# Transposed tokens from DRAM and a scaled row in place of TensorE transposes, in an attention and FFN kernel

## The chip, the core and the metric

The kernel runs on one core of a Trainium2 chip. The metric is device time in microseconds (us). Before the change it takes 655.53 us, the median of 3 runs (655.39 to 655.58).

A core has five engines that run at the same time, each with its own queue of instructions in order: TensorE (PE in the profile; its weight loads are PEld), VectorE (DVE), ScalarE (ACT), GpSimd (POOL) and SyncE (SP), which here issues DMAs. PE writes to PSUM banks; DVE and ACT read them.

## The reference

Tokens x are 2 x 2048 rows of D = 512. The context is 2 x 77 rows of 512. There are 16 heads of 32.

```
x = x + tanh(g_xattn) * (softmax(q k^T / sqrt(32)) v @ Wo^T + bo)
      q = layernorm(x) @ Wq^T + bq,  k = ctx @ Wk^T + bk,  v = ctx @ Wv^T + bv
      layernorm(x) = (x - mean) / sqrt(var + 1e-5), with no gain or bias
x = x + tanh(g_ffn) * qlinear(gelu(qlinear(layernorm(x), w1, b1)), w2, b2)
      qlinear(x, w, b) = (xq @ wq^T + b) * (sw * sx)
      xq, wq: rounded to 8 bits, one scale for each whole tensor
```

The query projection needs layernorm(x) with the 512 features on the partitions, while x comes with the tokens on the partitions.

## The kernel before

The 4096 tokens are 8 blocks of 512 (NB = 8, TB = 512), each of four tiles t of 128 tokens. Blocks are counted from 0 here, as in the code: x(0) to x(7). The first stage (lines 211 to 550) is attention in float32 for all blocks; the weights w1 and w2 are quantized beside it. The second stage (lines 570 to 638) computes the hidden layer in bf16, the third (lines 649 to 694) the output. The change touches only the first.

Loads are queued first (lines 115 to 136), most on SP: x of block 0, the key weights by groups of 128 columns, the query and value weights, the context, x of block 1. wk_sb and wv_sb live in buffers of the pool xblk, eight of 1 MB, through which x and the raw weight pieces of w1 and w2 also pass; a load waits on SP until its buffer is free.

*Before the loop* (lines 438 to 457) the orders of PE and DVE are written out by hand; ACT's is made by the compiler's planner. For block 0, tile by tile: statistics (layernorm_stats), 1/sigma on POOL (L163, a power of -0.5), transpose_x, and project_k(0, g), the keys of head group g for the first batch element. project_k multiplies wk by the context into a bank (pk) and then places 32 rows for each of four heads, with the bias added, into kblk: for b = 0 all four by ACT (L235), for b = 1 alternately by DVE (L237) and ACT.

*In the loop* (lines 463 to 523) PE's order alone is by hand; the planner orders the other engines from its costs and the order of the program. tc.issue_after(ins) puts the instructions of its block behind ins on the queue of the same engine. Each block i has eight steps s, two for each head group g. A step has, in PE's order:

- at even s, apply_v of the group before (pc, L345), which multiplies the transposed softmax by the values;
- softmax(i, s + 2), two steps ahead: scores ps on PE (L299), maximum mx and difference e on DVE (L308, L312), exponential on ACT (L318), sum and reciprocal on DVE (L320, L322), and the product e * rs on POOL (L323);
- transpose_a twice: PE transposes the softmax of step s (pta, L336), ACT copies it to aT (L337);
- at even s, project_o(i - 1, g) (po, L358), added to x by DVE (L365);
- at odd s, project_q: at 1 and 3 groups 2 and 3 of this block, at 5 and 7 groups 0 and 1 of the next (pq, L280, 8 records for four products of 128 features; copied with bias to qT by ACT, L288).

The layer norm of the next block runs beside this: norm(i + 1) at s = 1 (statistics on DVE, L159 to L162; 1/sigma on POOL, L163), and transpose_x(i + 1, t) for tiles 0 and 1 at the end of s = 3, for 2 and 3 at s = 5 ahead of the scores. transpose_x subtracts the mean and scales on DVE (xn, L266), transposes four 128x128 pieces on PE into a bank (ptx, L271), and copies them on ACT into xnT (L272).

In block 0 also: the keys and values of batch element 1 (project_k(1, s - 3) at s = 3 to 6, project_v(1) at 6). Other work of the loop: add_bias (L275, POOL), weight_step (maxima of w1 in block 1 and of w2 in block 3, quantization in 2 and 4, on DVE), and at s = 7 norm2_stats and norm2_max (DVE), the second layer norm of the block before. project_q, project_k, project_v, apply_v, project_o and scale_of share the PSUM pool ps_p, tag "pp", of two banks in turn. x of block i + 2 is queued on SP at the end of block i.

Of the kernel before, what the change touches and what calls it, by code (L numbers as in the profile page):

```python
# [15 lines left out]
P = 128  # L16
D = 512
# [25 lines left out]
def tile_flamingo_gated_block(  # L43
    ctx: ExitStack,
    tc: tile.TileContext,
    x: bass.AP,
    ctxT: bass.AP,
    g_xattn: bass.AP,
    g_ffn: bass.AP,
# [45 lines left out]
    ctx_sb = awts.tile([P, B, KC, NK], F32, name="ctx_sb")  # L95
# [3 lines left out]
    bv_sb = work.tile([NK, D], F32, tag="cT", name="bv_sb", bufs=7)  # L99
    bq_sb = const.tile([P, KC], F32, name="bq_sb")  # L100
    bk_sb = const.tile([P, KC], F32, name="bk_sb")
    tg = const.tile([P, 2], F32, name="tg")
# [7 lines left out]
        engine.dma_start(dst[:, :, c], kchunks(src)[:, :, c])  # L110

    def load_ctx(engine, b):
        engine.dma_start(ctx_sb[:, b, :, :], kchunks(ctxT[b]))

    load_x(0, pieces=NT, engines=(nc.sync, nc.scalar))
    load_ctx(nc.scalar, 0)
# [12 lines left out]
    for b in range(1, B):  # L129
        load_ctx(nc.sync, b)  # L130
    load_x(1)
    nc.sync.dma_start(wo_sb, kchunks(woT))
# [3 lines left out]
    nc.sync.dma_start(b1_sb, b1)  # L136

    ident = const.tile([P, P], F32, name="ident")
    make_identity(nc, ident)
# [71 lines left out]
    with actx:  # L211
# [7 lines left out]
        def project_k(b, g):  # L219

            pk = ps_p.tile([P, 512], F32, tag="pp", name=f"pk{b}_{g}")
            for kc in range(KC):
                nc.tensor.matmul(
                    pk[:, :NK],
                    wk_sb[:, kc, g * P : (g + 1) * P],
                    ctx_sb[:, b, kc, :],
                    start=(kc == 0),
                    stop=(kc == KC - 1),
                )
            for j in range(HG):  # L230
                r = slice(j * DK, (j + 1) * DK)
                dst = kblk[b][r, g, j % RT * NK : (j % RT + 1) * NK]
                bias = bk_sb[r, g : g + 1]
                if j % 2 or b == 0:
                    nc.scalar.activation(dst, pk[r, :NK], AF.Identity, bias=bias)  # L235
                else:
                    nc.vector.tensor_scalar(dst, pk[r, :NK], bias, None, ALU.add)  # L237

        def project_v(b):

            pv = ps_p.tile([P, 512], F32, tag="pp", name=f"pvv{b}")
            for kc in range(KC):
                nc.tensor.matmul(  # L243
                    pv[:NK, :],
                    ctx_sb[:, b, kc, :],
                    wv_sb[:, kc, :],
                    start=(kc == 0),
                    stop=(kc == KC - 1),
                )
            nc.vector.tensor_tensor(vblk[b], pv[:NK, :], bv_sb, ALU.add)  # L250

        ln, xnT, qT, aT, cT, es = {}, {}, {}, {}, {}, {}

        def norm(i):
# [3 lines left out]
            layernorm_stats(X[i], mv, rstd, f"a{i}")  # L258
            ln[i] = mv, rstd

        def transpose_x(i, t):
            mv, rstd = ln[i]
            if t == 0:
                xnT[i] = work.tile([P, KC, TB], F32, tag="xnT", name=f"xnT{i}", bufs=1)
            xn = work.tile([P, D], F32, tag="xn", name=f"xn{i}_{t}")
            nc.vector.tensor_scalar(  # L266
                xn, X[i][:, t, :], mv[:, t, 0:1], rstd[:, t : t + 1], ALU.subtract, ALU.mult
            )
            pt = ps_t.tile([P, KC, P], F32, tag="pt", name=f"ptx{i}_{t}")
            for kc in range(KC):  # L270
                nc.tensor.transpose(pt[:, kc, :], xn[:, kc * P : (kc + 1) * P], ident)  # L271
            nc.scalar.copy(xnT[i][:, :, t * P : (t + 1) * P], pt)  # L272
# [4 lines left out]
        def project_q(i, g):  # L277
            pq = ps_p.tile([P, TB], F32, tag="pp", name=f"pq{i}_{g}")
            for kc in range(KC):
                nc.tensor.matmul(  # L280
                    pq,
                    wq_sb[:, kc, g * P : (g + 1) * P],
                    xnT[i][:, kc, :],
                    start=(kc == 0),
                    stop=(kc == KC - 1),
                )
            qT[i, g] = work.tile([P, TB], F32, tag="qT", name=f"qT{i}_{g}", bufs=5)
            nc.scalar.activation(qT[i, g], pq, AF.Identity, bias=bq_sb[:, g : g + 1])  # L288

        def softmax(i, s):  # L290
# [144 lines left out]
                if j < 2:  # L435
                    load_w("w2", w2_piece, [j + 2])

        ordered = {mybir.EngineType.DVE, mybir.EngineType.PE}
        with tc.manual_schedule(engines=ordered):
            ln[0] = (  # L440
                small.tile([P, NT, 2], F32, tag="mv", name="mv0"),
                small.tile([P, NT], F32, tag="rstd", name="rstd0"),
            )
            for t in range(NT + 1):
# [12 lines left out]
            project_k(0, NG - 1)  # L457
        actx.enter_context(tc.manual_schedule(engines={mybir.EngineType.PE}))
        softmax(0, 0)
        softmax(0, 1)  # L460
        project_q(0, 1)
        project_v(0)
        for i in range(NB):
            for s in range(2 * NG):
                g, odd = divmod(s, 2)
                if not odd and s > 0:
                    apply_v(i, g - 1)
                elif not odd and i > 0:
                    apply_v(i - 1, NG - 1)
                if s == 5 and i + 1 < NB:  # L470
                    for t in (2, 3):
                        transpose_x(i + 1, t)
                if s + 2 < 2 * NG:
                    last = softmax(i, s + 2)
                elif i + 1 < NB:
                    last = softmax(i + 1, s + 2 - 2 * NG)
                for u in range(2):
                    transpose_a(i, s, u)
                if i == 0 and s == 2:


                    with tc.issue_after(last["ACT"]):
                        nc.scalar.activation(tg, tg, AF.Tanh)
                    with tc.issue_after(last["POOL"]):
                        nc.gpsimd.tensor_scalar(bo_sb, bo_sb, tg[:, 0:1], None, ALU.mult)
                if not odd and i > 0:
                    project_o(i - 1, g)
                if s in (1, 3):
                    project_q(i, g + 2)
                elif odd and i + 1 < NB:  # L490
                    project_q(i + 1, g - 2)
                if i + 1 < NB:
                    if s == 1:
                        with tc.issue_after(last["DVE"]):
                            norm(i + 1)
                    if s == 3:
                        for t in (0, 1):
                            transpose_x(i + 1, t)
                if i == 0 and 3 <= s < 7:
                    for b in range(1, B):  # L500
                        project_k(b, s - 3)
# [35 lines left out]
        xq0 = work.tile([P, NT, D], BF16, tag="xnT", name="xq0", bufs=1)  # L537
        for t in range(NT):
            v, vq = xs0[:, t, :], xq0[:, t, :]
            if t < NT // 2:  # L540
# [216 lines left out]
```

## Time and profile before

| | us |
|---|---|
| median of 3 runs | 655.53 |
| the profiled execution | 655.2 |
| its span, first to last instruction | 653.3 |
| xn on DVE (L266), 32 operations, mean 0.66 | 20.4 |
| transposes of x on PE (ptx, L271), 128 | 18.4 |
| copies of them on ACT (L272), 32 | 17.3 |
| query projection on PE (L280), 256 records | 115.4 |
| softmax product on POOL (L323), 64 of 1.23 | 78.6 |

The profile is of one execution. "Busy" counts an instruction's own duration; matmuls overlap, so their durations add up to more than the path they take. In a list of groups, a line reads: source line, engine, operation, what is written <- what is read, shapes, count, busy time and mean; in a timeline: start, length, the same names, and in brackets how long the engine was idle before and which instruction released it. The mean granted TensorE clock is 0.987 of full speed.

### The profile page before, as it was taken

To read this page: it belongs to the slowest core of one execution; us is meant where nothing else is said; L and a number is where in the kernel's file an instruction comes from. 1 tells how busy PE (TensorE), PEld (TensorE's weight loads), DVE (VectorE), ACT (ScalarE), POOL (GpSimd) and SP (SyncE) were. 2 spreads that over 40 slices of the span, in tenths; PEclk is the share of its full clock that TensorE was granted. 3 is DMA by queue.
4 is the path that set the end of the run, shared out by engine and by line. 5 is a ranking of instruction groups with operands and counts; after the bars stand their busy time and mean duration, and the time that the engine had idled before them with its cause. 6 is when DMAs were issued, how large, how long until landed. Compare 5 with 4: busy or idle time off the path is not lost.

```text
span 653.3 us, 8220 instructions
## 1 busy us (share of the span) xinstructions
PE 625.0 (96%) x3048; PEld 317.4 (49%) x3048; DVE 514.7 (79%) x809; ACT 342.8 (52%) x479; POOL 204.1 (31%) x161
## 2 busy tenths in 40 slices
PE   5999999999999999999999999599999979999997
PEld 4565555455554554555555543244444434444443
DVE  3586687998998998976877768899999788887551
ACT  4465444444444354354344441399999979544430
POOL 2144333234343334233242331000000009996000
PEclk9999999999999999999999999699999989999999
DMA  9902000031131131100000000089999109789952
GB/s 281 376 34 93 37 1 1 2 129 65 65 130 68 62 129 64 66 1 0 1 2 0 2 18 0 19 295 319 333 323 329 25 8 359 273 325 345 334 207 80
DMA packets 44255, 84.90 MB, mean 130 GB/s; under 512 B 18795, under 2 KB 22891, under 8 KB 38584
## 3 DMA queue, kind: packets, MB, share of 16 engines
q1 hardware_dynamic: 43112, 83.70, 36.5%
q10 hardware_dynamic: 1104, 0.69, 0.3%
q8 instruction: 24, 0.39, 0.3%
q14 instruction: 15, 0.12, 0.1%
HBM read 49.25 MB, written 31.46 MB: 124 GB/s over the span
## 4 chain that ended last, share of the span: by engine, by line
PE 85%; DVE 11%; ACT 2%; issue 1%; DMA 1%; POOL 0%; ACTq 0%; DVEq 0%
PE pf L674 17%; PE ph L610 17%; PE po L358 15%; PE pq L280 14%; PE pta L336 8%; PE ps L299 6%; PE pc L345 4%; PE ptx L271 2%; DVE tm L380 1%; DVE xf L189 1%; PE pvv L243 1%; DVE mx L308 1%; DVE e L312 1%; DVE sm L320 1%; DVE max_w L401 1%
## 5 line engine op out<-in xcount | busy, mean ns | idle before, releaser
L323 POOL TENSOR_TENSOR e<-e,rs 128x616 f32<-128x616 f32 x64 | 78.6, 1229 | 223.3 <-DVE rs L322 149.1
L280 PE MATMUL pq<-xnT,wq_sb 128*128 128x512 f32 x256 | 115.4, 593 | 0.9 <-ACT xnT L272 0.9
L674 PE MATMUL pf<-w2q,hq 128*128 128x512 bf16 x512 | 113.6, 385 | 2.3 <-DVE hq L205 2.0
L358 PE MATMUL po<-wo_sb,cT 128*128 128x512 f32 x256 | 114.8, 593 | 0.0
L610 PE MATMUL ph<-xqT,w1q 128*128 128x512 bf16 x512 | 112.1, 382 | 0.7 <-DVE xqT L550 0.7
L617 ACT ACTIVATE G<-ph,b1s,s 128x512 f32<-128x512 f32 x128 | 99.6, 778 | 14.1 <-PE ph L610 3.3
L337 ACT COPY aT<-pta 77x512 f32<-77x512 f32 x128 | 68.1, 582 | 69.2 <-PE pta L336 69.2
L318 ACT ACTIVATE e<-e 128x616 f32<-128x616 f32 x64 | 45.9, 717 | 85.8 <-DVE e L312 84.3
L627 DVE TENSOR_REDUCE hmax<-G 128x1 f32<-128x1024 f32 (+1 forms) x65 | 76.8, 1198 | 7.0 <-ACT G L617 6.9
L674 PEld LDWEIGHTS <-hq 128*128 128x128 bf16 x512 | 50.7, 99 | 64.9 <-issue 3.6
L610 PEld LDWEIGHTS <-w1q 128*128 128x128 bf16 x512 | 50.4, 99 | 62.2 <-issue 1.9
L336 PE MATMUL pta<-ident,e 128*77 128x128 f32 x512 | 70.2, 280 | 0.4 <-ACT xnT L272 0.4
L358 PEld LDWEIGHTS po<-wo_sb,cT 128*128 128x128 f32 x256 | 46.4, 190 | 48.2 <-issue 46.6
L320 DVE TENSOR_REDUCE sm<-e 128x8 f32<-128x616 f32 x64 | 50.6, 790 | 24.4 <-ACT e L318 24.1
L308 DVE TENSOR_REDUCE mx<-ps 128x8 f32<-128x616 f32 x64 | 50.2, 784 | 24.4 <-PE ps L299 23.9
L280 PEld LDWEIGHTS pq<-xnT,wq_sb 128*128 128x128 f32 x256 | 46.1, 190 | 47.1 <-issue 46.1
L667 ACT ACTIVATE Gb<-Gb,inv_h 128x2048 f32<-128x2048 f32 x22 | 43.7, 2001 | 36.8 <-DMA Gb<-h 32.5
L336 PEld LDWEIGHTS pta<-ident,e 128*77 128x77 f32 x512 | 55.6, 147 | 11.8 <-issue 10.3
L299 PEld LDWEIGHTS ps<-kb,qT 64*128 64x128 f32 x512 | 36.0, 186 | 43.5 <-ACT qT L288 20.6
L688 POOL TENSOR_TENSOR x<-x,b_sb 128x512 f32<-128x512 f32 x32 | 56.2, 1794 | 0.1
L312 DVE TENSOR_TENSOR e<-ps,mx 128x616 f32<-128x616 f32 x64 | 50.9, 796 | 2.4
L299 PE MATMUL ps<-kb,qT 64*128 64x154 f32 x512 | 50.6, 317 | 0.3 <-ACT qT L288 0.2
(89 smaller groups left out, 590.6 us busy)
## 6 DMA issues: line engine op xcount, KB each, us to landing
h<-G SPq DMA_DIRECT2D x22, 1024.0 KB, 5.9
Gb<-h SPq DMA_DIRECT2D x22, 1024.0 KB, 7.9
raw_w<-in_w2T SPq DMA_DIRECT2D x8, 1024.0 KB, 5.2
out_y<-x SPq DMA_DIRECT2D x32, 256.0 KB, 2.8
x<-in_x SPq DMA_DIRECT2D x7, 1024.0 KB, 5.5
raw_w<-in_w1T SPq DMA_DIRECT2D x4, 1024.0 KB, 12.6
wk_sb<-in_wkT SPq DMA_DIRECT2D x4, 256.0 KB, 5.2
wq_sb<-in_wqT SPq DMA_DIRECT2D x4, 256.0 KB, 6.2
```

The source lines that it names most:

```text
L280: nc.tensor.matmul(pq, wq_sb[:, kc, g * P : (g + 1) * P], xnT[i][:, kc, :], start=(kc == 0), stop=(kc == KC - 1),)
L299: nc.tensor.matmul(ps[:, q, u * RK : (u + 1) * RK], qT[i, g][r, t * P : (t + 1) * P], kblk[i // NBB][r, g, :], start=True, stop=True,)
L312: last["DVE"] = nc.vector.tensor_tensor(e.rearrange("p u (q r k) -> p q u r k", q=NR, r=RT), sc, mx[:, :, :, :, None].to_broadcast([P, NR, ...
L320: nc.vector.tensor_reduce(sm, e4, AX.X, ALU.add)
L323: last["POOL"] = nc.gpsimd.tensor_tensor(e4, e4, rs[:, :, :, None].to_broadcast([P, 2, HG, NK]), ALU.mult).ins
L336: nc.tensor.transpose(pt[:NK, j, :], es[i, s][:, u, j, :], ident)
L337: nc.scalar.copy(aT[i, g][:, :, t * P : (t + 1) * P], pt[:NK, :, :])
L358: nc.tensor.matmul(po, cT[i, g][:, t * P : (t + 1) * P], wo_sb[:, g, :], start=(g == 0), stop=(g == NG - 1),)
L610: nc.tensor.matmul(ph, w1q[:, kc, fc * P : (fc + 1) * P], cur[:, kc, :], start=(kc == 0), stop=(kc == KC - 1),)
L617: nc.scalar.activation(G[:, 2 * v + u, :], ph, AF.Gelu, bias=b1s[:, fc : fc + 1], scale=s1,)
L627: nc.vector.tensor_reduce(hmax[:, k + u : k + u + 1], G[:, 2 * v + u : 2 * v + u + n, :], AX.XY, ALU.max, apply_absolute_value=True,)
L674: nc.tensor.matmul(po[t], hq[:, fc, t * P : (t + 1) * P], w2q[:, fc, :], start=(fc == 0), stop=(fc == FC - 1),)
```

## The change

The host also gives x transposed (xT, 512 x 4096). For blocks 1 to 7:

- load_xT brings the block, features on the partitions, into xT_sb, in buffers of the tag xnT, now two;
- norm writes the four columns of 1/sigma to a row in DRAM and reads that row back into all 128 partitions (rrow), both DMAs on SP; it is called at s = 0, in block 0 at s = 1 as before;
- scale_x multiplies xT_sb by the row in place on POOL, four operations of 128x512, two at s = 2 and two at s = 3 (in block 0 at 3 and 4), each pair behind that step's softmax product;
- the mean is not subtracted from x; center_wq (block 0, s = 3, after the last query projection of block 0) takes from the query weights their mean over the features instead: three additions on POOL, one product with ones on PE (bank pm of "pp"), four operations on DVE that read pm and write wq_sb.

So transpose_x is left only for block 0. Before the loop ACT's order is by hand too, the keys of b = 0 are placed by DVE, and key group 2 is multiplied before the first query projection. The context lives in two buffers of the tag cT; qT has four buffers, not five. x and xT of block i + 2 are queued at s = 6.

```
+    def load_xT(i):
+        xT_sb[i] = work.tile([P, KC, TB], F32, tag="xnT", name=f"xT{i}", bufs=2)
+        nc.sync.dma_start(xT_sb[i], kchunks(xT[:, i * TB : (i + 1) * TB]))
...
-                if j % 2 or b == 0:
+                if j % 2 and b > 0:
                     nc.scalar.activation(dst, pk[r, :NK], AF.Identity, bias=bias)
                 else:
                     nc.vector.tensor_scalar(dst, pk[r, :NK], bias, None, ALU.add)
...
+            row = rows.tile([NT, P], F32, tag="row", name=f"row{i}")
+            nc.sync.dma_start(row.rearrange("t p -> p t"), rstd)
+            rstd_row[i] = work.tile([P, TB], F32, tag="rrow", name=f"rrow{i}", bufs=1)
+            nc.sync.dma_start(
+                rstd_row[i], row.rearrange("(o t) p -> o (t p)", o=1).to_broadcast([P, TB])
+            )
+
+        def scale_x(i, kc):
+
+            xs = xT_sb[i][:, kc, :]
+            nc.gpsimd.tensor_tensor(xs, xs, rstd_row[i], ALU.mult)
+
+        def center_wq():
+
+            total = work.tile([P, D], F32, tag="xn", name="wq_total")
+            nc.gpsimd.tensor_tensor(total, wq_sb[:, 0, :], wq_sb[:, 1, :], ALU.add)
+            for kc in range(2, KC):
+                nc.gpsimd.tensor_tensor(total, total, wq_sb[:, kc, :], ALU.add)
+            pm = ps_p.tile([P, D], F32, tag="pp", name="pm")
+            nc.tensor.matmul(pm, ones, total, start=True, stop=True)
+            for kc in range(KC):
+                w = wq_sb[:, kc, :]
+                nc.vector.scalar_tensor_tensor(w, pm, -1.0 / D, w, ALU.mult, ALU.add)
...
-                    xnT[i][:, kc, :],
+                    (xnT if i == 0 else xT_sb)[i][:, kc, :],
...
-        ordered = {mybir.EngineType.DVE, mybir.EngineType.PE}
+        ordered = {mybir.EngineType.DVE, mybir.EngineType.PE, mybir.EngineType.Activation}
...
-                if t > 1:
-                    project_k(0, t - 2)
+                if t in (2, 3):
+                    pk[t - 2] = project_k(0, t - 2)
+            place_k(0, 0, pk[0])
+            pk[2] = project_k(0, 2)
+            place_k(0, 1, pk[1])
             project_q(0, 0)
-            project_k(0, NG - 1)
+            place_k(0, 2, pk[2])
+            pk[3] = project_k(0, 3)
+            place_k(0, 3, pk[3])
...
-                if s == 5 and i + 1 < NB:
-                    for t in (2, 3):
-                        transpose_x(i + 1, t)
...
-                    if s == 1:
+                    first = 1 if i == 0 else 0
+                    if s == first:
                         with tc.issue_after(last["DVE"]):
                             norm(i + 1)
-                    if s == 3:
-                        for t in (0, 1):
-                            transpose_x(i + 1, t)
+                    if s in (first + 2, first + 3):
+                        with tc.issue_after(last["POOL"]):
+                            for kc in range(2 * (s - first) - 4, 2 * (s - first) - 2):
+                                scale_x(i + 1, kc)
+                    if i == 0 and s == 3:
+                        center_wq()
...
+                if s == 6 and i + 2 < NB:
+                    load_x(i + 2)
+                    load_xT(i + 2)
...
-            if i + 2 < NB:
-                load_x(i + 2)
```

More of the change, by code (lines that the diff above doesn't have):

```diff
@@ L46, in tile_flamingo_gated_block @@
     x: bass.AP,
+    xT: bass.AP,
     ctxT: bass.AP,
@@ L94, in tile_flamingo_gated_block @@
     wo_sb = awts.tile([P, KC, D], F32, name="wo_sb")
-    ctx_sb = awts.tile([P, B, KC, NK], F32, name="ctx_sb")
     kblk = [awts.tile([P, NG, RK], F32, name=f"kb{b}") for b in range(B)]
@@ L99, in tile_flamingo_gated_block @@
     bv_sb = work.tile([NK, D], F32, tag="cT", name="bv_sb", bufs=7)
+    ctx_sb = [work.tile([P, KC, NK], F32, tag="cT", name=f"ctx{b}", bufs=7) for b in range(B)]
     bq_sb = const.tile([P, KC], F32, name="bq_sb")
@@ L112, in load_ctx @@
     def load_ctx(engine, b):
-        engine.dma_start(ctx_sb[:, b, :, :], kchunks(ctxT[b]))
+        engine.dma_start(ctx_sb[b], kchunks(ctxT[b]))
     load_x(0, pieces=NT, engines=(nc.sync, nc.scalar))
@@ L131, in tile_flamingo_gated_block @@
     load_x(1)
+    xT_sb = {}
+    def load_xT(i):
+        xT_sb[i] = work.tile([P, KC, TB], F32, tag="xnT", name=f"xT{i}", bufs=2)
+        nc.sync.dma_start(xT_sb[i], kchunks(xT[:, i * TB : (i + 1) * TB]))
     nc.sync.dma_start(wo_sb, kchunks(woT))
@@ L136, in tile_flamingo_gated_block @@
     nc.sync.dma_start(b1_sb, b1)
+    rows = ctx.enter_context(tc.tile_pool(name="rows", bufs=2, space=bass.MemoryType.DRAM))
     ident = const.tile([P, P], F32, name="ident")
@@ L225, in project_k @@
                     wk_sb[:, kc, g * P : (g + 1) * P],
-                    ctx_sb[:, b, kc, :],
+                    ctx_sb[b][:, kc, :],
                     start=(kc == 0),
@@ L229, in project_k, with place_k @@
                 )
+            return pk
+        def place_k(b, g, pk):
             for j in range(HG):
@@ L244, in project_v @@
                     pv[:NK, :],
-                    ctx_sb[:, b, kc, :],
+                    ctx_sb[b][:, kc, :],
                     wv_sb[:, kc, :],
@@ L250, in project_v @@
             nc.vector.tensor_tensor(vblk[b], pv[:NK, :], bv_sb, ALU.add)
+        rstd_row = {}
         ln, xnT, qT, aT, cT, es = {}, {}, {}, {}, {}, {}
@@ L263, in transpose_x @@
             if t == 0:
-                xnT[i] = work.tile([P, KC, TB], F32, tag="xnT", name=f"xnT{i}", bufs=1)
+                xnT[i] = work.tile([P, KC, TB], F32, tag="xnT", name=f"xnT{i}", bufs=2)
             xn = work.tile([P, D], F32, tag="xn", name=f"xn{i}_{t}")
@@ L286, in project_q @@
                 )
-            qT[i, g] = work.tile([P, TB], F32, tag="qT", name=f"qT{i}_{g}", bufs=5)
+            qT[i, g] = work.tile([P, TB], F32, tag="qT", name=f"qT{i}_{g}", bufs=4)
             nc.scalar.activation(qT[i, g], pq, AF.Identity, bias=bq_sb[:, g : g + 1])
@@ L443, in tile_flamingo_gated_block @@
             )
+            pk = {}
             for t in range(NT + 1):
@@ L453, in tile_flamingo_gated_block @@
                     transpose_x(0, t - 1)
-                if t > 1:
-                    project_k(0, t - 2)
+                if t in (2, 3):
[3 more added lines that the diff above has]
+            place_k(0, 1, pk[1])
             project_q(0, 0)
-            project_k(0, NG - 1)
+            place_k(0, 2, pk[2])
+            pk[3] = project_k(0, 3)
+            place_k(0, 3, pk[3])
         actx.enter_context(tc.manual_schedule(engines={mybir.EngineType.PE}))
+        load_xT(1)
         softmax(0, 0)
@@ L492, in tile_flamingo_gated_block @@
                 if i + 1 < NB:
[L493 removed]
+                    first = 1 if i == 0 else 0
+                    if s == first:
                         with tc.issue_after(last["DVE"]):
                             norm(i + 1)
[L496 to L498 removed]
+                    if s in (first + 2, first + 3):
[4 more added lines that the diff above has]
+                        center_wq()
                 if i == 0 and 3 <= s < 7:
                     for b in range(1, B):
[L501 removed]
+                        place_k(b, s - 3, project_k(b, s - 3))
                         if s == 6:
@@ L536, in tile_flamingo_gated_block @@
         s_x, inv_x = scale_of(diagonal_of(xmax, "x"), "x", ps_p, "pp")
-        xq0 = work.tile([P, NT, D], BF16, tag="xnT", name="xq0", bufs=1)
+        xq0 = work.tile([P, NT, D], BF16, tag="xnT", name="xq0", bufs=2)
         for t in range(NT):
@@ L727 @@
         "x": x.reshape(-1, D),
+        "xT": x.reshape(-1, D).T,
         "ctxT": np.asarray(ctx_1024).transpose(0, 2, 1),
```

## The prediction

> **What bounds the kernel now.** I read the page's busy shares first, then its 40 slices, then the stages around the change, then TensorE's order of work in one block.
>
> ```profile
> PE 625.0 (96%) x3048; PEld 317.4 (49%) x3048; DVE 514.7 (79%) x809; ACT 342.8 (52%) x479; POOL 204.1 (31%) x161
> PE   5999999999999999999999999599999979999997
> DVE  3586687998998998976877768899999788887551
> ```
>
> TensorE (PE) is busy 96% of the span and is full from slice 1 to slice 23, which is the attention part. So there a removed TensorE instruction should shorten the time. The stage table (start and end, then length, and for each engine busy us and instructions) says the same and shows the neighbours:
>
> ```profile
> 0.00:20.00 20.00, 11.89 (x62) 9.35 (x64) 6.08 (x18) 8.45 (x20) 4.54 (x13) 1.00 1.00 297
> 150.00:200.00 50.00, 49.96 (x253) 25.91 (x251) 46.48 (x77) 22.21 (x38) 17.73 (x14) 1.00 0.23 85
> ```
>
> Columns are PE, PEld, DVE, ACT, POOL. In 150 to 200 us PE works 49.96 of 50 us, but VectorE (DVE) is close behind with 46.48, so DVE's lag has to be watched. POOL has room (17.73). The first 20 us hold 8 us of idle PE. TensorE's timeline in block 1 prices the transposes that go:
>
> ```profile
> 75.45 3.60 PE L280 MATMUL pq<-xnT,wq_sb 128*128 128x512 f32 x8
> 78.98 1.06 PE L345 MATMUL pc<-aT,vb 77*32 77x512 f32 x8
> ...
> 86.82 3.60 PE L280 MATMUL pq<-xnT,wq_sb 128*128 128x512 f32 x8
> 90.26 1.04 PE L271 MATMUL ptx<-ident,xn 128*128 128x128 f32 x8
> 91.23 1.07 PE L345 MATMUL pc<-aT,vb 77*32 77x512 f32 x8
> 93.88 3.60 PE L358 MATMUL po<-wo_sb,cT 128*128 128x512 f32 x8
> 97.32 1.04 PE L271 MATMUL ptx<-ident,xn 128*128 128x128 f32 x8
> 98.28 0.79 PE L299 MATMUL ps<-kb,qT 64*128 64x154 f32 x8
> ```
>
> From pq to pc takes 3.53 us without transposes (75.45 to 78.98) and 4.41 with eight (86.82 to 91.23): eight transposes cost 0.88 us of the path. With po the figures are 4.40 and 3.52 (81.64 to 85.16), again 0.88. An instruction's own 0.27 us is no price; the distance is.
>
> **What the Trainium skill says.** "TensorE: Matmul & The Clock Gate", Part 2 (step 5): the drain of one matmul overlaps the fill of the next, so a stream costs spacing, not latency. The trace agrees: 0.11 us per transpose by distance. "GPSIMD Engine Reference", 3.1: a two-input elementwise operation takes about 2.6 cycles an element at 1.2 GHz, an estimate of 1.1 us plus dispatch for 512. The trace has the same shape as what scale_x does, the bias add of L275, at 1.27 us; I use that. "DMA: Bandwidth & Descriptors", Rules for kernel authors: a non-contiguous last dimension becomes one descriptor per element, so the row of 512 values goes out as 512 descriptors; no such store is in the trace. "Advanced Engine Details and Errata", VectorE Performance Modes: GpSimd and VectorE's two-port mode block each other. The trace fits: xn (L266) takes 0.49 to 1.44 us.
>
> **The change part by part.** The profiled execution took 655.2 us with a span of 653.3; the median of the runs is 655.53, 0.3 above, so I take the sum off 655.5.
>
> *Transposes, blocks 1 to 6 (for x of blocks 2 to 7).* Two groups of 0.88 us a block: 6 x 1.76 = **-10.6 us**, all on PE's path. With them go four xn per block on DVE (0.66 us each) and four copies on ACT (0.59), beside PE.
>
> *GpSimd scaling.* Four operations of 1.27 us a block, 5.1 us on POOL. POOL then does 8 x 1.22 + 4 x 1.27 + 2 x 1.28 + 5.1 = 22.5 us in a block of about 45.6 (47.3 now, less 1.76). Free if they don't delay the softmax products (L323), which PE transposes next. These lines are of block 3; its step 5 transposes start at 194.79:
>
> ```profile
> 184.54 1.22 POOL L323 TENSOR_TENSOR e<-e,rs 128x616 f32<-128x616 f32 x1 [2.75 <-DVE rs L322]
> 185.72 1.28 POOL L275 TENSOR_TENSOR x<-x,bo_sb 128x512 f32<-128x512 f32 x1
> 190.03 1.31 POOL L323 TENSOR_TENSOR e<-e,rs 128x616 f32<-128x616 f32 x1 [3.04 <-ACT aT L337]
> 194.79 1.10 PE L336 MATMUL pta<-ident,e 128*77 128x128 f32 x8
> ```
>
> The first product is of softmax step 4, behind which the first pair of scale_x is queued; the second is of step 5, with 194.79 - 191.34 = 3.4 us to spare. A pair (2.5 us) fits into the gap 185.8 to 190.0 if the row of 1/sigma is there.
>
> *The row: norm one step earlier, two DMAs on SP.* In block 3 norm may start after e at 170.34, so at 171.1; now it starts at 174.24 and its ve_a ends at 180.70, 6.5 us. The row then follows: 177.6, rstd on POOL 1.3 (L163), store and load with two issues of 0.5. The store is unseen: 2.8 us is the landing of a 256 KB store (out_y), 5.0 to 6.2 that of the 2 KB loads bq and bk at a busy time; I take 3.5. The load into 128 partitions: 3.3, as b_sb's 256 KB. The row lands at about 186.8. The latest harmless time: product 5 must end by 194.79 - 0.88 = 193.9, less 1.3 and a pair 2.5, so 190.1. Margin 3.3 us. Not every block will have it: DVE has norm2's 3.6 us of statistics and about 5 us of maxima just before, and the w2 pieces (5.2 us to land) share SP and the DMA engines. I put 0.3 us on each of six blocks, **+1.8** (bounds 0 and the rival below). A gain below nothing is excluded: nobody waits for POOL to be busier.
>
> *Block 0.* Step 3: project_q(0,3), then the new pm matmul, pk, then pc. The pool "pp" has two banks, so pc takes pm's bank and waits for four DVE operations that read it. As L365 (0.74 us with a PSUM input) they need 2.9 us. From the end of pq: pm is one 128x512 f32 product (two records at 0.44), done at +1.05; four operations to +4.0, with 0 to 2.6 us of softmax work in front. Now pc comes 0.88 + 0.86 = 1.8 us after pq. So pc comes 2.2 to 4.8 us later; I take **+3.2**, the removed first group counted. Behind pc wait ps and all else on PE. The three adds of GpSimd (3 x 1.27) need only the loaded weights, and POOL idles before 24.57 us, so they cost nothing; placed at step 3 they would add about 4 us. Step 5: a group of 0.88 goes, with the 0.36 us wait before pta at 50.10: **-1.2**. But project_q(1,0) needs the second pair of scale_x, queued behind the product of softmax(0,6). Now ps of that softmax starts at 45.47 and its product ends at 51.7, +6.2; the pair ends at +8.7. project_q would start at +4.2 (51.01 - 45.47, less 1.32) and wants its last quarter at +6.9: **+1.8** (0 to 2.5). Together +3.8.
>
> *The first keys.* Now copy x of the last tile waits behind kb on ACT: pq starts at 15.08, after the copy of 14.44 to 15.03. With kb on DVE (0.29 us each, idle there from 10.8) the copy can follow its transposes at 13.4 and end at 14.0; PE does pk 2 first, to about 14.1. So pq starts about 14.1: **-1.0** (0 to -1.2; nothing if the loads are late, the DMA share being 1.00 there).
>
> *Loads.* xT adds 7 MB and the row loads 1.8 MB. The DMA share is 0.10 to 0.23 in the middle, and an x block lands in 5.5 us. The first xT is queued on SP before x of block 2 and the w1 pieces, whose first maximum is taken only at 79.6 us; a later x moves from the end of a block to step 6, with its xT behind it, and is wanted two steps (2 x 5.9 us) later. Nothing, at 0.4 us an issue. With ctx, three of cT's seven buffers are held in block 0, where cT fills one every other step; of qT's four at most three are alive. Nothing.
>
> Sum: -10.6 + 1.8 + 3.8 - 1.0 = **-6.0**, so 649.5 us.
>
> **Rivals.** *All is hidden* (chance 0.18): DVE takes pm's operations at once and the row is early. Then -10.6 - 1.0 and block 0 at about -1, so 643. For it: between 40 and 360 us PE now idles under 2 us, so the engines around it do keep up. Against it: pp has only two banks.
>
> *DVE takes the bound* (0.13): norm at step 0 falls into DVE's densest stretch. In block 3 the ps of step 0 ends at 165.08 and its mx starts at 169.52, 4.4 us late. If DVE's lag grows by the 3.6 us of norm there, PE waits about 1 us a block: -6.0 + 5 = about 654.5. Against it: over a block DVE loses 2.2 to 2.6 us, PE only 1.76.
>
> *The row comes late* (0.17), the slower one: POOL stands at scale_x waiting for the row, and the softmax products stand behind it. With norm ending no earlier than now (180.7), and DMAs of 5.0 and 5.2, the row lands at 180.7 + 1.3 + 11.2 = 193.2, 3.1 us past 190.1. In the five blocks with norm2 ahead (2 to 6) this is 15.5 us: 649.5 + 15.5 = 665. The decision point is 6.0 / 5 = 1.2 us past the limit, 191.3. That SP has a waiting weight load ahead of the row (it is in-order) would do the same.
>
> **How the numbers follow.** Forecast 649.5 (own range 646.5 to 652), 0.52; all hidden 0.18; DVE bound 0.13; late row 0.17. 0.2% (1.3 us) is about what the measurement can tell. Of the DVE case about half (0.06) is still faster. So faster 0.76, same 0.07, slower 0.17. The range 642.5 to 656.5 leaves out most of the late row and little else.
>
> **What would show it.** Period of blocks 5 and 6 (pc to pc, now 47.3) at 45.5 to 45.9. A PE wait before pc at step 3 of block 0 put down to the new DVE operation, 2 to 5 us. A wait in the first pq of block 1 for scale_x. The first pq at 14.1. Waits of pta for POOL stay under 3 us in all. The prediction is wrong if POOL shows long waits for the row's DMA with pta behind them, or if mx lags further in steps 0 to 2.

## The result, and the profile after

The changed kernel takes 673.05 us, the median of 4 runs (671.87 to 676.7), against 655.56 (4 runs) for the kernel before on the same chip: a ratio of 1.027 (95% interval 1.0255 to 1.029), slower. The profiled execution took 673.24 us with a span of 671.5, so it is 18.2 us of span that have to be found. The forecast was 649.5, its range 642.5 to 656.5.

The page of the kernel after, TensorE's busy row and then the slices of TensorE, of VectorE and of the granted TensorE clock:

```profile
PE 625.2 (93%) x2938; PEld 313.0 (47%) x2938; DVE 509.7 (76%) x801; ACT 323.8 (48%) x435; POOL 243.3 (36%) x192
...
PE   5999999998997998997989999599999979999997
...
DVE  5675677996985996973866867899998878888541
...
PEclk9998999998998998998999999789999998999999
```

110 records went from TensorE, yet its busy time is the same, since others took longer (the transposes of the softmax 0.292 us each on the mean, 0.280 before), and its row, full of nines in slices 1 to 23 before, has holes now: slices 9, 12, 15 and 18 in blocks 2 to 5, and 20 in block 6. At the first four VectorE and the clock have a dent in the same slice, at slice 20 the clock has none. A dent of VectorE suggests that it waits too; the lists of waits below decide that. The stage table (start and end, length, then PE, PEld, DVE, ACT, POOL, each with its instructions, then clock, DMA share and GB/s) says it in numbers:

```profile
0.00:20.00 20.00, 12.63 (x51) 10.13 (x51) 9.62 (x30) 3.63 (x5) 6.05 (x15) 1.00 1.00 293
150.00:200.00 50.00, 45.70 (x221) 23.83 (x218) 42.04 (x68) 19.13 (x32) 23.20 (x18) 0.97 0.29 101
```

From 150 to 200 us TensorE works 45.70 of 50 us (49.96 before). A block is measured from the first apply_v (pc) of one block to that of the next. Undisturbed, block 1 shows what the removal is worth. TensorE's timeline has the pc at the start of block 1 and the one at the start of block 2, first in the kernel before:

```profile
67.61 1.06 PE L345 MATMUL pc<-aT,vb 77*32 77x512 f32 x8
...
114.84 1.06 PE L345 MATMUL pc<-aT,vb 77*32 77x512 f32 x8
```

and then in the kernel after, with the second pc of block 1 between them:

```profile
73.86 1.07 PE L382 MATMUL pc<-aT,vb 77*32 77x512 f32 x8
...
85.23 1.06 PE L382 MATMUL pc<-aT,vb 77*32 77x512 f32 x8
...
119.35 1.06 PE L382 MATMUL pc<-aT,vb 77*32 77x512 f32 x8
```

114.84 - 67.61 = 47.23 us, and 119.35 - 73.86 = 45.49 us. All blocks, from the same lines of both kernels (and of the best version, which comes last in the experiments):

| block | 1 | 2 | 3 | 4 | 5 | 6 |
|---|---|---|---|---|---|---|
| before, us | 47.23 | 48.45 | 47.34 | 48.44 | 47.36 | 47.23 |
| after, us | 45.49 | 51.62 | 51.30 | 51.03 | 51.34 | 47.48 |
| last experiment, us | 45.50 | 46.69 | 46.44 | 46.70 | 45.49 | 45.49 |

Blocks 2 and 4 hold 1.2 us more in all three kernels (the scale of a weight, pg_w). Beyond that and 45.49, blocks 2 to 5 after are 4.92, 5.81, 4.33 and 5.85 us too long: 20.9 us. The lists of waits, TensorE's and GpSimd's (us in total, times, longest), give the first reason:

```profile
PE pta L373 <- POOL e L360: 15.0, 5, 4.4
...
PE ps L336 <- ACT qT L325: 2.1, 2, 1.9
...
PE pc L382 <- DVE wq_sb L296: 1.5, 1, 1.5
...
PE pq L317 <- POOL xT L284: 0.8, 1, 0.8
```

```profile
POOL xT L284 <- DMA rrow<-row: 46.8, 7, 9.6
```

TensorE waits 15.0 us for the softmax product, and GpSimd waits 46.8 us for the row, once for each of the seven blocks of x that it scales. TensorE waits behind it in blocks 2 to 5 only; one of its five waits, 0.9 us in block 3, stays in runs where the row is early (below). Why the row is late stands in the list of DMA issues (the last number is the median time from issue to landing):

```profile
rrow<-row SPq DMA_DIRECT2D x7, 256.0 KB, 5.9
...
row<-rstd SPq DMA_DIRECT2D x7, 2.0 KB, 8.3
```

The store of 2 KB takes longer than the load of 256 KB. Block 2 in the timeline, from 1/sigma to the transposes that wait:

```profile
132.41 1.02 POOL L171 TENSOR_TENSOR rstd<-ve_a,mhalf 128x4 f32<-128x4 f32 x1
133.46 0.36 SPq L275 DMA_DIRECT2D row<-rstd  x1
141.81 0.33 SPq L277 DMA_DIRECT2D rrow<-row  x1
148.78 2.49 POOL L284 TENSOR_TENSOR xT<-xT,rrow 128x512 f32<-128x512 f32 x2 [6.54 <-DMA rrow<-row]
149.24 0.20 DVE L359 RECIPROCAL rs<-sm 128x8 f32<-128x8 f32 x1
151.22 1.26 POOL L312 TENSOR_TENSOR x<-x,bo_sb 128x512 f32<-128x512 f32 x1
152.44 1.22 POOL L360 TENSOR_TENSOR e<-e,rs 128x616 f32<-128x616 f32 x1
153.72 1.99 PE L373 MATMUL pta<-ident,e 128*77 128x128 f32 x8 [3.43 <-POOL e L360]
```

The load is issued only when the store has landed, 8.35 us after it (141.81 - 133.46), and the pair of scale_x starts 6.97 us later: 15.3 us from the end of 1/sigma. The product's own input rs was ready at 149.44; it runs 3.0 us later, because the pair and a bias add are ahead of it on GpSimd's queue. TensorE stands still for 3.43 us. And there is a second reason in the last line: the eight transposes take 1.99 us instead of 1.10. TensorE comes back from the wait at a lower clock. In the table of stretches (columns as in the stage table), the clock stands at 0.50 for these 2 us:

```profile
153.70:155.70 2.00, 1.99 (x9) 1.99 (x10) 1.04 (x1) 0.58 (x1) 2.00 (x1) 0.50 0.95 350
```

The sum from the trace: before block 0's first pc +1.2; block 0 +5.05; transposes -1.74 in each of six blocks, -10.4; the excess of blocks 2 to 5 +20.9; block 6 another +2.0; the rest of the kernel -0.3. Together +18.4, against 18.2 measured.

### The profile page after: what moved, and what is told of

Same layout as the page of the kernel before. It is cut to its first block, busy times and chain, and to the rows that moved or that the text cites. A ratio compares the mean times of both kernels' runs of the same rounds, so it can differ in the third digit from the quotient of the medians.

```text
span 671.5 us, 8017 instructions
## 1 busy us (share of the span) xinstructions
PE 625.2 (93%) x2938; PEld 313.0 (47%) x2938; DVE 509.7 (76%) x801; ACT 323.8 (48%) x435; POOL 243.3 (36%) x192
## 2 busy tenths in 40 slices
DMA packets 52654, 94.07 MB, mean 140 GB/s; under 512 B 22715, under 2 KB 26811, under 8 KB 46984
## 4 chain that ended last, share of the span: by engine, by line
PE 65%; DVE 24%; POOL 4%; issue 4%; ACT 2%; DMA 1%; POOLq 0%; DVEq 0%; ACTq 0%
PE pf L720 17%; PE ph L656 16%; PE po L395 9%; PE pq L317 8%; PE pta L373 6%; PE ps L336 3%; DVE e L349 3%; DVE mx L345 3%; PE pc L382 3%; DVE xf L197 2%; DVE sm L357 2%; DVE tm L417 2%; DVE st_a L167 2%; DVE x L402 1%; DVE st_f L167 1%
## 5 line engine op out<-in xcount | busy, mean ns | idle before, releaser
L663 ACT ACTIVATE G<-ph,b1s,s 128x512 f32<-128x512 f32 x128 | 99.5, 777 | 14.1 <-PE ph L656 3.2
L317 PE MATMUL pq<-xT,wq_sb 128*128 128x512 f32 x224 | 103.5, 604 | 0.9 <-POOL xT L284 0.8
L373 PE MATMUL pta<-ident,e 128*77 128x128 f32 x512 | 74.7, 292 | 15.0 <-POOL e L360 15.0
L373 PEld LDWEIGHTS pta<-ident,e 128*77 128x77 f32 x512 | 59.3, 155 | 26.8 <-POOL e L360 17.7
L317 PEld LDWEIGHTS pq<-xT,wq_sb 128*128 128x128 f32 x224 | 41.6, 197 | 42.9 <-issue 39.2
L284 POOL TENSOR_TENSOR xT<-xT,rrow 128x512 f32<-128x512 f32 x28 | 36.9, 1338 | 46.8 <-DMA rrow<-row 46.8
L336 PE MATMUL ps<-kb,qT 64*128 64x154 f32 x512 | 51.2, 320 | 2.1 <-ACT qT L325 2.1
```

Of the source, the lines that this page charges most:

```text
L317: nc.tensor.matmul(pq, wq_sb[:, kc, g * P : (g + 1) * P], (xnT if i == 0 else xT_sb)[i][:, kc, :], start=(kc == 0), stop=(kc == KC - 1),)
L336: nc.tensor.matmul(ps[:, q, u * RK : (u + 1) * RK], qT[i, g][r, t * P : (t + 1) * P], kblk[i // NBB][r, g, :], start=True, stop=True,)
L373: nc.tensor.transpose(pt[:NK, j, :], es[i, s][:, u, j, :], ident)
L663: nc.scalar.activation(G[:, 2 * v + u, :], ph, AF.Gelu, bias=b1s[:, fc : fc + 1], scale=s1,)
```

## The experiments

The theory after the result: the row of 1/sigma is late, since its store takes 8.3 us, and GpSimd's waiting scale_x holds up the softmax product. The rivals: VectorE's denser order at step 0 makes everything late and the row's wait is only where it shows; the wait itself is harmless and the 2.5 us of scaling in front of the product is what costs; and the size of the row, not the form of its store, makes the round trip slow.

**Norm a step earlier (e1_norm_early).** The row is asked for earlier instead of being made faster.

```
-                    if s == first:
+                    if i == 0 and s == 1:
                         with tc.issue_after(last["DVE"]):
-                            norm(i + 1)
+                            norm(1)
+                if s == 7 and i + 2 < NB:
+                    with tc.issue_after(last["DVE"]):
+                        norm(i + 2)
...
+                if s == 4 and i + 2 < NB:
+                    load_x(i + 2)
                 if s == 6 and i + 2 < NB:
-                    load_x(i + 2)
                     load_xT(i + 2)
```

> norm of block i + 2 moves to step 7 of block i (two steps of a block earlier than in the change: it was called at step 0 of block i + 1, and DVE finished it at about step 2), and the load of x to step 4; norm(1) stays. Late row (theory): the row lands before step 2, POOL's waits for it in blocks 1 to 6 go to nearly nothing, PE's 15.0 us of waits for the softmax product and the slow-clock stretches behind them go, and the time falls by about 20 us to 650 to 654. GpSimd's own work (rival): the 5.1 us of scaling a block are unchanged, so the time stays above 668. DVE (rival): norm is now ahead of norm2 in the densest stretch of DVE, so the time stays at 673 or rises.

Measured: 676.26 us, ratio 1.032 (1.0294 to 1.0346). A miss. The row's wait is gone in all blocks but block 0 (GpSimd waits once, 6.8 us), but norm and norm2 now stand together at step 7. Timeline of this kernel, VectorE and then TensorE in the next block:

```profile
127.48 0.99 DVE L197 TENSOR_SCALAR xf<-x,mean,rstd 128x512 f32<-128x512 f32 x2
128.39 1.27 DVE L417 TENSOR_REDUCE tm<-xf 128x1 f32<-128x512 f32 x2
129.58 0.28 DVE L179 TENSOR_SCALAR diag_w<-ident,m_w 128x128 f32<-128x128 f32 x1
130.00 0.77 PE L186 MATMUL pg_w<-diag_w,ones 128*128 128x128 f32 x2 [5.94 <-DVE xmax L421]
```

The small product pg_w of a weight's scale waits 5.94 us for diag_w, which VectorE does only after norm2's xf and tm, and the same happens in block 4. Blocks 3 and 5 take 51.2 and 51.3 us, with a wait of 1.9 us for the exponential in each. So late VectorE work is a real cost where norm is put into a dense stretch, but here it took the place of the row's wait: this run says nothing against the late row, and doesn't show what the row costs.

**No wait for the row (e2_no_row_wait).** scale_x multiplies by bo_sb, which has long been there. It leaves out 1/sigma; instructions and DMAs stay the same.

```
-            nc.gpsimd.tensor_tensor(xs, xs, rstd_row[i], ALU.mult)
+            nc.gpsimd.tensor_tensor(xs, xs, bo_sb, ALU.mult)
```

> Both DMAs of the row stay, but GpSimd scales xT by bo_sb, which is there from the start, in place of the row; 1/sigma is left out of the queries of blocks 1 to 7. All work of POOL, DVE and the DMA queues is kept, only the wait for the row is taken away. Late row: about 650 (673 less the 22.9 us that blocks 2 to 6 lost beyond their transposes). GpSimd's own work or DVE's lag: 668 to 673, since nothing of either changed.

Measured: 654.29 us in one run, span 652.5: 19.0 us of span less than after, with norm still at step 0. TensorE's waits of this kernel:

```profile
PE ps L336 <- ACT qT L325: 1.8, 2, 1.6
...
PE pta L373 <- POOL e L360: 0.9, 1, 0.9
```

Of the 15.0 us 0.9 is left, in block 3. So VectorE's order at step 0 isn't the cause, and four operations a block of GpSimd's scaling are hidden as priced. What is missing to 649.5 is in block 0 (36.32 us), in block 6 (3.4 us above 45.49) and at the head, which is 2.6 us longer than in the kernel before.

**The wait without the work (e3_wait_only).** scale_x multiplies one column of 512, so it waits for the row as before but holds GpSimd for 0.33 us a pair, not 2.49. It leaves out the scaling of the other columns.

```
-            nc.gpsimd.tensor_tensor(xs, xs, rstd_row[i], ALU.mult)
+            nc.gpsimd.tensor_tensor(xs[:, 0:1], xs[:, 0:1], rstd_row[i][:, 0:1], ALU.mult)
```

> scale_x waits for the row as in the change but multiplies one column of each chunk only, so the queries of blocks 1 to 7 lack 1/sigma in nearly all tokens; GpSimd has almost none of the 5.1 us of scaling a block left. Late row: POOL still waits about 45 us for the row; the product behind it comes 2.5 us earlier, so PE's waits of 3 to 4 us shrink to about 1 and the clock no longer falls: 655 to 662. GpSimd's own work: the loss goes entirely, 646 to 650. DVE: 673.

Measured: 654.34 us in one run, span 652.5, just below what was expected of the late row (655 to 662) and far above the 646 to 650 of GpSimd's own work. TensorE's and GpSimd's waits of this kernel:

```profile
PE pta L373 <- POOL e L360: 4.5, 4, 2.0
```

```profile
POOL xT L284 <- DMA rrow<-row: 45.1, 7, 9.3
```

GpSimd still waits 45.1 us for the row, and TensorE only 4.5. Blocks 2 to 5 take 47.47, 47.41, 46.83 and 49.24 us: of the 20.9 us too many, 6.6 are left with the wait alone, and 0.9 with the work alone (e2). Most of the loss needs both: work that has been held back by a wait runs in front of the product just when that is due.

**The row stored as it lies (e4_row_16B).** 1/sigma lies as 128 partitions x 4 values. The change stores it in the order of the tokens, as 512 pieces of 4 bytes; here each partition's four values go out as one piece of 16 bytes. The values then stand in another order, so tokens get each other's 1/sigma.

```
-            row = rows.tile([NT, P], F32, tag="row", name=f"row{i}")
-            nc.sync.dma_start(row.rearrange("t p -> p t"), rstd)
+            row = rows.tile([P, NT], F32, tag="row", name=f"row{i}")
+            nc.sync.dma_start(row, rstd)
...
-                rstd_row[i], row.rearrange("(o t) p -> o (t p)", o=1).to_broadcast([P, TB])
+                rstd_row[i], row.rearrange("(o p) t -> o (p t)", o=1).to_broadcast([P, TB])
```

> The row is stored as it lies, 16 bytes from each partition (128 pieces in place of 512 of 4 bytes), and read back in that order, so tokens take each other's 1/sigma. If the 8.3 us of the store are paid by piece: it lands in about 3.5 to 4.5 us, the row comes 4 us earlier, PE's waits for the product fall from 15 to under 3 us, and the time is 652 to 656. If the 8.3 us are fixed (a write to DRAM and its acknowledgment): the store stays at 8 us and the time at 670 to 675.

Measured: 652.63 us in one run, span 650.8: 20.7 us less than after. The DMA issues of this kernel, and TensorE's wait:

```profile
rrow<-row SPq DMA_DIRECT2D x7, 256.0 KB, 4.5
...
row<-rstd SPq DMA_DIRECT2D x7, 2.0 KB, 1.4
```

```profile
PE pta L373 <- POOL e L360: 0.9, 1, 0.9
```

The same 2 KB land in 1.4 us. The profile counts 49966 DMA packets in this kernel and 52654 in the changed one, 2688 fewer, which is 7 x (512 - 128): the pieces are as the layouts say. Blocks 2 to 5 take 46.70, 46.43, 46.70 and 45.50 us. The 0.9 us of block 3 stay with the row early (here and in e2), so the late row accounts for 20.9 - 0.9 = 20.0 us of the changed kernel.

**A quarter of the row (h1_quarter_row).** Only tile 0's 1/sigma is stored, 128 pieces of 4 bytes, and all four tiles are scaled by it, so the 1/sigma of the other three is left out. It parts the number of pieces from their size.

```
-            nc.sync.dma_start(row.rearrange("t p -> p t"), rstd)
+            nc.sync.dma_start(row.rearrange("o p -> p o"), rstd[:, 0:1])
...
```

> Only tile 0's 1/sigma is stored (128 pieces of 4 bytes in place of 512), read back into 128 partitions as 512 bytes each, and used for all four tiles of a block. The mended row has 128 pieces of 16 bytes and lands in 1.4 us, the change's 512 pieces of 4 bytes in 8.3. If the number of pieces sets the landing: 1.4 to 2.2 us. If the size of 4 bytes does: about 8. The time falls to about 652 in the first case and stays near 670 in the second.

Measured: 665.92 us in one run, span 664.1. DMA issues and TensorE's wait:

```profile
rrow<-row SPq DMA_DIRECT2D x7, 64.0 KB, 5.5
...
row<-rstd SPq DMA_DIRECT2D x7, 0.5 KB, 7.1
```

```profile
PE pta L372 <- POOL e L359: 9.4, 5, 3.3
```

With the same number of pieces as e4 (the packets are 49966 in both) and a quarter of its bytes, the store takes 7.1 us at the median. Four times as many add 1.2. So it is stores in pieces of 4 bytes that are slow here, not 512 of them. A shorter row would have mended little: 1.2 us of 8.3.

**The head alone (f1_head_only).** The kernel before with only the new order of the first keys (project_k split into place_k, VectorE places, group 2 multiplied before the first query projection, ACT's order by hand before the loop).

> The kernel before with the edit ahead of the loop alone: the first keys placed by DVE, ACT's order by hand, key group 2 ahead of the first query projection. By the prediction's step: 1.0 us faster (ratio 0.9985), the first query projection starting at 14.1. If what the profile of the changed kernel shows is of the edit (TensorE stays at half clock some 4 us longer, first query projection at 16.0): 1 to 2 us slower (1.002 to 1.003). If the later clock is chance: no difference beyond the interval.

Measured: 655.08 against 655.71, ratio 0.9989 (0.998 to 0.9999), so -0.7 us (0 to -1.3). The price of 1.0 lies within that interval. But in its profile the first query projection starts at 15.03 us, against 15.08 before and not at 14.1, so the profile doesn't show where the gain comes from.

**The row mended (f2_row_mended).** As e4, but with every token's own value: GpSimd reads the row with a step of four elements.

```
-            xs = xT_sb[i][:, kc, :]
-            nc.gpsimd.tensor_tensor(xs, xs, rstd_row[i], ALU.mult)
+            xs = xT_sb[i][:, kc, :].rearrange("a (t p) -> a t p", t=NT)
+            r = rstd_row[i].rearrange("a (p t) -> a t p", t=NT)
+            nc.gpsimd.tensor_tensor(xs, xs, r, ALU.mult)
```

> The row is stored with 16 bytes from each partition, and GpSimd reads it back in the token order of xT by a step of four elements, so the computation is that of the reference. If the store's pieces were the cause and the strided read costs GpSimd nothing: 652 to 653.5, with scale_x at 1.27 us. If the strided read doubles scale_x to 2.5 us (10 us a block): POOL delays the product again by 2 to 3 us in five blocks, 660 to 668.

Measured: 653.03 us, ratio 0.9961 (0.9942 to 0.998): faster than before, and 20.0 us less than the change. The group of scale_x in this kernel (shortest, median and longest ns of one):

```profile
L285 POOL TENSOR_TENSOR xT<-xT,rrow x28: 1507/1530/2568, 44.6 to 331.4; 128x512 f32<-128x512 f32 x28
```

The step costs 0.26 us an operation (1.53 at the median, against 1.27 for the same operation in e4), which is hidden. The six runs lie between 650.89 and 655.74, so differences of a microsecond or two between single runs mean nothing here. 3.5 us are still missing to 649.5.

**norm2 elsewhere (f3_norm2_later).** f2, with norm2 of the block before not at step 7 but at step 3 of the block after, to clear VectorE before block 6's scores.

```
-                if s == 7 and i > 0:
+                if s == 3 and i > 1:
+                    norm2_stats(i - 2)
+                    norm2_max(i - 2)
+                if s == 7 and i == NB - 1:
                     norm2_stats(i - 1)
                     norm2_max(i - 1)
```

> As the run with the mended row, and norm2 of block i - 1 moves from step 7 of block i to step 3 of block i + 1, where the x scaling was taken from DVE (the last two stay as they must). If DVE's lag around steps 7 to 1 is what makes PE wait for qT in block 6 (1.92 us and a slow clock behind it, 3.7 in all) and about 0.9 in others: 648 to 650. If that lag is without effect: as the mended row.

Measured: 653.44 us, ratio 0.9964 (0.9947 to 0.998). A miss: nothing gained over f2. TensorE's waits:

```profile
PE ps L337 <- ACT qT L326: 5.1, 3, 1.8
```

The wait left block 6 and came back three times, at 142.72, 237.43 and 250.43 us, in blocks 2 and 4, where the quantization of a weight shares VectorE with norm2. Block 6 takes 45.50 us, blocks 2 and 4 49.22 and 49.16.

**Block 0 mended (f4_block0, on f3; f5_row_block0, on f2).** center_wq goes from step 3 to step 1 and norm(1) with its row and scalings one step ahead.

```
-                    if i == 0 and s == 3:
+                    if i == 0 and s == 1:
                         center_wq()
...
-                    first = 1 if i == 0 else 0
+                    first = 0
```

> As the run before it, and in block 0 the centring goes from step 3 to step 1 (behind the query projection of group 2; the next use of its PSUM bank is at step 3) and norm(1) from step 1 to step 0. If block 0 lost time by that bank (1.5 us) and by waiting for the second pair of scale_x (0.8 to 1.2 us and a slow clock): 2 to 4 us less than the run before it, 645 to 647.5. If the loss in block 0 has another cause: the same as the run before it.

> The mended row with block 0's two moves (centring at step 1, norm(1) at step 0), and norm2 where the change has it, at step 7. Moving norm2 took PE's waits for qT out of block 6 (3.7 us with the slow clock) but brought them into blocks 2 and 4, where the quantization shares step 3 (6.6 us of waits): with norm2 back, 1 to 3 us less than the 650.4 of the run with all three, 648 to 649.5. If the block 0 moves alone made that gain: 2.5 to 3 us less than the mended row alone, 650 to 650.5.

Measured: f4 650.45, ratio 0.9918 (0.9906 to 0.993), 3.0 less than f3; f5 649.44, ratio 0.9894 (0.9877 to 0.9911), 3.6 less than f2 (in a later comparison, in which the kernel before took 655.86 us, not 655.71). The difference came as expected both times; f4's own time missed since f3 had. Block 0's waits for wq_sb and xT are gone; one of 1.65 us for the softmax product is there instead. The block takes 32.65 us in f5 (68.54 - 35.89) against 32.80 before and 37.85 after.

**norm2 moved in the last blocks alone (f6_row_block0_norm2).** f5 shows whose wait block 6 has. Timeline of f5, VectorE, ACT and TensorE:

```profile
311.48 0.79 DVE L350 TENSOR_TENSOR e<-ps,mx 128x616 f32<-128x616 f32 x1
312.36 0.72 ACT L356 ACTIVATE e<-e 128x616 f32<-128x616 f32 x1 [4.33 <-DVE mean L168]
312.99 0.67 ACT L326 ACTIVATE qT<-pq,bq_sb 128x512 f32<-128x512 f32 x1
313.71 0.79 PE L337 MATMUL ps<-kb,qT 64*128 64x154 f32 x8 [1.91 <-ACT qT L326]
```

The difference e comes late from VectorE, which has norm2's last maxima and then norm's statistics in front of it; the exponential waits for it on ACT; the copy of qT stands behind the exponential in ACT's order though its own input, pq, was done by 310.8 us; TensorE waits for qT. Of blocks 1 to 6 of f5, only block 6 has the two in this order. At the same place in block 5 the copy comes first:

```profile
265.35 0.69 ACT L326 ACTIVATE qT<-pq,bq_sb 128x512 f32<-128x512 f32 x1 [1.85 <-PE pq L318]
...
268.03 0.72 ACT L356 ACTIVATE e<-e 128x616 f32<-128x616 f32 x1 [1.07 <-DVE mean L168]
```

There the exponential is late too, and TensorE doesn't wait for qT. So the wait could go by taking VectorE's lag away, or perhaps by turning the order on ACT, which wasn't tried. For the first, norm2 is moved only where no quantization shares step 3:

```
+                if s == 3 and i > NB - 3:
+                    norm2_stats(i - 2)
+                    norm2_max(i - 2)
-                if s == 7 and i > 0:
+                if s == 7 and (0 < i < NB - 3 or i == NB - 1):
```

> As the run before it, with norm2 at step 3 of the next block in blocks 6 and 7 alone, where no weight is quantized. If DVE's lag in block 6 is what holds qT on ACT (1.9 us and the slow clock behind it): 3 to 3.7 us less than the run before it, 645 to 646.5. If not: the same as it.

Measured: 645.91 us, ratio 0.9847 (0.9825 to 0.987), 3.5 less than f5. It beats both kernels. The exponential is still ahead of the copy at that place, but VectorE is done with e in time, and TensorE's wait is gone. TensorE's slices and its stage:

```profile
PE   5998999999999999999999997799999979999997
```

```profile
150.00:200.00 50.00, 49.13 (x252) 25.38 (x252) 45.31 (x74) 21.45 (x36) 26.06 (x20) 1.00 0.39 122
```

The nines are back, and the blocks stand in the table above: all at 45.49, save the weight scales and block 3's 0.9.

## Why the prediction was wrong

**The row** is the step that failed: "The row: norm one step earlier, two DMAs on SP", priced at +1.8 and measured at +20.0. Its mechanism was right, that GpSimd does the scaling for nothing if the row is there in time; three of its terms were mis-sized, the store above all.

- The store. It was unseen before, and 3.5 us was taken from a 256 KB store (2.8) and from 2 KB loads (5.0 to 6.2). It took 8.3. None of those had pieces of 4 bytes. The list of DMA issues of the kernel before has two that do, and they were passed over:

```profile
b_sb<-in_b SPq DMA_DIRECT2D x1, 256.0 KB, 3.3
...
bk_sb<-in_bk ACTq DMA_DIRECT2D x1, 2.0 KB, 6.2
...
tg<-in_g_xattn SPq DMA_DIRECT2D x1, 0.5 KB, 8.0
tg<-in_g_ffn SPq DMA_DIRECT2D x1, 0.5 KB, 7.3
```

tg is one value of 4 bytes for each of 128 partitions, bk 16 bytes for each. They are loads, at a busy time, so they don't price a store; but b_sb's 256 KB, issued behind tg, landed in 3.3, and a bound of 8 us could be read from tg, while the late-row rival went no higher than 5.0. The Trainium skill, "DMA: Bandwidth & Descriptors", Specifications, says that a transfer under 512 B makes the engine read, modify and write; no run here shows that step, and it would put 16 bytes with 4, while the runs part them: 1.4 us and 8.3.

- The load. 3.3 was taken; it took 5.9 in the changed kernel and 4.5 in e4. In the changed kernel x, xT and a weight piece can stand right behind it on SP (below); whether they slow it wasn't tried.
- What a late row costs. The text counted only the time that TensorE waits. After each wait of 2.8 to 4.4 us the clock was down, and about 1.5 us more was lost (block 2: excess 4.92, wait 3.43; block 5: 5.85 and 4.42). In the four blocks that is 5.9 of the 20.0 us. The same skill, "TensorE: Matmul & The Clock Gate", Part 1, says that the clock is halved after at least one idle window of about 3.4 us; the trace has the half clock (0.50, and 1.99 us for 1.10), but already after the wait of 2.76, so here the measurement decides.

Against that, norm itself was quicker than priced: in block 2 from its first statistics (127.56) to the end of 1/sigma (133.43) 5.9 us, not 7.8. Without that the row would have been later still.

**The rival** "the row comes late" had the mechanism word for word: GpSimd stands at scale_x, the products stand behind it. Its waits were nearly right: 15.5 us in five blocks, against 14.1 in four (15.0 less the 0.9 that isn't the row's). At 665, in which the +1.8 of the row is still contained, it is 8 us short: 3.6 us more in blocks 2 to 5, mostly the clock, block 6, and the head and block 0. Its chance of 0.17 was the error of judgement: the decision point was 1.2 us past the limit, and the margin of 3.3 us hung on one term that had been borrowed from transfers of another kind.

**Transposes, blocks 1 to 6**: right. -1.74 a block against -1.76, in block 1 of the changed kernel and in every undisturbed block.

**GpSimd scaling**: hidden as said (e2), as long as the row is early. An operation took 1.27 us at the median, as priced.

**Block 0**: +5.05 against +3.8. The steps were right, the sizes not. The pc of step 3 waits for the new VectorE work as foretold, 1.54 us, and comes 1.8 us later than before, not 3.2: the four operations took 2.5 us in all, with no softmax work in front of them. From there to the next pc it is 3.3 us more than before, where +0.6 was priced (-1.2 and +1.8). project_q(1, 0) waits for the second pair, 0.77. In e4 the same stretch is 0.6 more, as priced. What is above that is the clock. These are the pc at step 3 in the timeline, of the kernel after and then of e4:

```profile
47.45 1.94 PE L382 MATMUL pc<-aT,vb 77*32 77x512 f32 x8 [1.54 <-DVE wq_sb L296]
```

```profile
47.48 1.07 PE L382 MATMUL pc<-aT,vb 77*32 77x512 f32 x8 [1.54 <-DVE wq_sb L296]
```

The wait is the same; in the one the clock falls (0.50 from 47.4 to 54.2 us), and work that takes 3.6 us in the other takes 6.7. At the next pc 2.7 us of that are left. So this term is uncertain by nearly 3 us for the same order of work, and a range for it should have said so. That it is the edits of block 0 and not the row is shown by f2 and f5: 3.6 us.

**The first keys**: f1 has -0.7 for -1.0. In the profiled run of the changed kernel the head is +1.2: pk at 14.35 us still takes 1.82 us, while the one at 19.81 takes 1.01. That looks like the half clock, though the granted clock reads 1.00 there. In other profiles with this head the first query projection began anywhere from 14.14 to 16.05 us. Why TensorE came to full speed when it did wasn't settled.

**DVE takes the bound**: not at step 0. With norm there, blocks 1 to 5 of f5 take 45.49, 46.70, 46.44, 46.70 and 45.49 us, weight scales and block 3's 0.9 included. But block 6 has it in a small way, +2.0 us after and +3.6 in e4: a wait of 1.92 us in both, and in e4 the clock behind it. It takes norm2 at step 7, norm at step 0 and ACT's order of the two operations together; the rival had only the second of these, and about 1 us in every block.

**Loads**: nothing, as said, for TensorE. But SP is in order: in block 2 x, xT and the w2 piece are issued at 142.24 to 145.18, right behind the row's load, which waited 8 us for its store. The lists of waits have no engine that waits for xT or a w2 piece, and for x only at the start.

So -10.4 was there to have. The plan lost it, and more, mainly by the form of one store, and with the store, block 0 and block 6 mended the kernel gains 10.0 us (655.86 to 645.91 in one comparison), and ends 3.6 below the forecast.

## What to carry to other kernels

Before a step leans on a small store, look at the size of its pieces in memory and at the time from issue to landing, not at its bytes: here a layout that follows the partitions took 1.4 us, and the one in the order of the tokens 8.3. A wait on an engine off the critical path costs what is queued behind it: put the waiting work behind what the bounding engine needs next, or make sure that its input is early by more than the least known term of its price. In a kernel like this one, count for every TensorE wait of two us or more another 1.5 us for the clock. Where a step has no row in the profile, look for one with pieces of the same size, and let the chance of the rival that hangs on it be no smaller than the chance that the row you borrowed is of the wrong kind.

## What the runs showed of the hardware

- From issue to landing, a store to DRAM of 4-byte pieces took 8.3 us (512 pieces) or 7.1 (128 pieces), and one of 128 pieces of 16 bytes 1.4. Loads of 128 pieces of 4 bytes took 8.0 and 7.3 us in the kernel before, at a busy time. Why 4 bytes are so slow wasn't tried: here neighbouring pieces come from different partitions, which could matter.
- The eight transposes after a TensorE wait took 1.99 us after waits of 2.76 to 4.42, 1.91 and 1.83 after 2.39 and 3.27 (h1), 1.79 after 1.99 (e3), and 1.10 after 0.7 to 1.67 where no other wait was near. In these seven cases of 1.99 us and over, the block lost 1.4 to 1.8 us beyond the wait. After waits of 1.5 to 2 us the clock fell in some cases and not in others: block 0's wait of 1.54 was followed by a clock of 1.00 in e4 and of 0.50 in the changed kernel, and block 6's wait of 1.92 cost 0.1 us more in the changed kernel and 1.7 in e4.
- GpSimd's product of two 128x512 operands took 1.53 us with one of them read in steps of 16 bytes (f2), and 1.27 with both dense (e4).
